# An expert's fourth block of outputs issued at the beginning of the next attention step, with the third norm's transposes ordered behind it

## The chip, the cores and the metric

The kernel runs on one core of a Trainium2 chip. Its time is the device time of one execution in microseconds (us). Five engines work side by side, each through its own instructions in their order: TensorE (PE, with its weight loads shown apart as PEld), VectorE (DVE), ScalarE (ACT), GpSimd (POOL) and SyncE (SP, which here only issues DMAs). They wait for each other by semaphores.

## What is computed

Two layers over 128 graphs of 64 nodes, 8192 nodes of 256 features in all, in float32. Each layer is a graph block and a feed-forward block, both with a residual:

```python
x = x + _L0_gnn_ref(_layernorm(x), adj, ...)     # graph convolution, softplus
x = x + _L0_ffn_ref(_layernorm(x), ...)          # 8 experts, the best one per node
x = x + _L1_gnn_ref(_layernorm(x), adj, ...)     # graph attention
x = x + _L1_ffn_ref(_layernorm(x), ...)          # 4 experts, the best two per node
...
def _L1_gnn_ref(h, adj, W, a, gamma, beta):
    Wh = jnp.matmul(h, W)
    e = s1[:, :, None] + s2[:, None, :]          # s1, s2 = Wh @ a1, Wh @ a2
    e = jnp.where(e > 0, e, ALPHA * e)
    e = jnp.where(adj > 0, e, NEG)
    attention = jax.nn.softmax(e, axis=2)
    h_prime = jnp.matmul(attention, Wh)
    return gelu(layernorm(h_prime) * gamma + beta)
...
    for ei in range(NUM_EXPERTS):                # in _L1_ffn_ref
        hh = jax.nn.gelu(x @ W1[ei] + b1[ei], approximate=False)
        out = out + g[..., None] * (hh @ W2[ei] + b2[ei])
```

The gate `g` of the last block comes from an attention over a list of 1,048,576 edges, whose sums need every node's row; so it is known late.

## The kernel before

The 8192 nodes are 64 tiles of 128, and four tiles are a group (16 groups). x stays on the chip throughout. The stages follow each other: layer 0's graph block and routing, layer 0's experts, then **attention's steps** (the stage of this change), then the edge list, and last the routed and remaining experts.

**The steps.** Attention runs in 26 steps (line 1322). In step s up to five generators, called streams, work each on its own group, so that a group passes through them in order: `back` (group s: fetches layer 0's expert rows by an indirect DMA on POOL, adds them to x on DVE, line 1168), `first` (group s-4: first norm, transposes, the products with W, the scores `ee`), `second` (group s-5: exponential `pb` on ACT line 1232, transposes of it on PE line 1236, copied to `pT` by ACT line 1238, the attention product on PE line 1243, copied into `ring` by ACT line 1244, then its statistics and `eps` on DVE lines 1145 and 1248), `combine` (group s-7: second norm on DVE lines 1260 and 1261, gelu, added to x), and `tables` (group s-10: third norm `z` on DVE line 1044, transposes on PE line 1184, copied to `zT` by ACT line 1185, stored, and eight small products for the edge list, line 1281). The streams take turns, one piece each per round r. At the end of every second step `make_factors` works out the norms' factors for two steps (the `mf` operations on DVE, lines 162 to 166, 1302, 1307 and 153 to 158).

**The units.** Beside the streams the last block's experts are already at work, on groups whose third norm is done: they fill TensorE's idle time, and what they make is stored in `ystore` until the gates are known. The generator `experts` hands out units of work. A hidden block is two products of 128x512 (line 1074) and a gelu on ACT (line 1078). An output block is four products of 128x256 into one `py` (line 1084, into the PSUM tile `pw`, of which there are two, shared with `first`), an addition of the bias on DVE (line 1088, into `yin`, of which there are six, shared with the rows that `back` fetches) and a store issued on SP (line 1111). An expert of a group is four hidden blocks and then four output blocks. In the profile each product of float32 shows as two matmul records, so an output block is eight records.

**The quota.** A line in the step loop says how many units are issued after each round of the streams. With at = s - 12, a step with an even `at` issues four units after the third round (the four hidden blocks of an expert), one with an odd `at` two after the first round and two after the second (its four output blocks). From step 21 on it is one after each of the first three rounds:

```python
                if s >= NG + SECOND:
                    quota = int(r < 3)
                elif at >= 0:
                    quota = (2 * (at % 2), 2 * (at % 2), 4 - 4 * (at % 2), 0, 0, 0, 0, 0)[r]
```

**The order.** The program is written as a stream of operations; a scheduler, at build time, decides each engine's order of instructions by priority (earlier written goes first) and by its own idea of what is ready, and sets the semaphores. `tc.issue_after(ins)` adds an edge for the scheduler alone: the instructions of its block come behind `ins` on the same engine.

Of the kernel before, what the change touches and what calls it, by code (L numbers as in the profile page):

```python
# [20 lines left out]
P = 128  # L21
# [3 lines left out]
GR = 4  # L25
# [3 lines left out]
FIRST, SECOND, COMBINE, TABLES = 2 * PART, 2 * PART + 1, 3 * PART + 1, 4 * PART + 2  # L29
RING = COMBINE - SECOND + 1  # L30
NG = NT // GR
# [49 lines left out]
def kernel(  # L81
# [31 lines left out]
    nc = tc.nc  # L113
# [30 lines left out]
    ident = const.tile([P, P], F32, name="ident")  # L144
# [273 lines left out]
    with tc.tile_pool(name="w0", bufs=1, reuse_waits="tile") as w0, tc.tile_pool(name="kp", bufs=1, reuse_waits="tile") as kp:  # L418
# [29 lines left out]
        with tc.tile_pool(name="b2", bufs=2, reuse_waits="tile") as b2, tc.tile_pool(name="bh", bufs=NH + 2, reuse_waits="tile") as bh, tc.tile_pool(  # L448
# [4 lines left out]
            def transposed(zT, z, k):  # L453
                tz = psb.tile([P, GR * P], F32, name="tz")[:, 0:D].rearrange("p (c n) -> p c n", c=2)
                for c in range(2):
                    nc.tensor.transpose(tz[:, c, :], z[:, c * P : c * P + P], ident)
                S.copy(zT[:, :, k * P : k * P + P], tz)
# [408 lines left out]
            with tc.tile_pool(name="bs", bufs=3, reuse_waits="tile") as bs, tc.tile_pool(  # L866
# [11 lines left out]
                steps, counts = keys.finish(bm), keys.count()  # L878
                zt_rows = zrows.rearrange("(s p) f -> s p f", p=P)
                why = "there are E0 experts, and no tile of theirs is past the last"  # L880

                def load(g):
# [23 lines left out]
                def turned(zs):  # L906
                    zT = b2.tile([P, 2, GR * P], F32, name="zT")
                    for k, z in enumerate(zs):
                        transposed(zT, z, k)
                    return zT  # L910
# [99 lines left out]
    def load_weights():  # L1010
        for e in range(NEXP):
            nc.sync.dma_start(w1[:, e], f1_w1[e].rearrange("(c p) f -> p c f", p=P))
            nc.sync.dma_start(w2[:, e], f1_w2[e].rearrange("(q p) f -> p q f", p=P))
        nc.sync.dma_start(b1, f1_b1.rearrange("e (q p) -> p e q", p=P))
        for t, of in ((b2, f1_b2.rearrange("e f -> (e f)")), (bgat, f1_bgat), (lng, f1_lng), (lnb, f1_lnb)):
            nc.sync.dma_start(t, row(of).to_broadcast(t.shape))
# [22 lines left out]
    def scaled(dst, src, g, norm, k):  # L1039
        scale, shift, mean = factors(g, norm, k)  # L1040
        if norm == 0:
            S.activation(dst, src, AF.Identity, bias=shift, scale=scale)
        else:
            V.tensor_scalar(dst, src, mean, scale, ALU.subtract, ALU.mult)
# [15 lines left out]
    adds = []  # L1060
    n_kept = [0] * DENSE
    pace = []
    sums = []
    behind = []

    def experts(g, take):

        zT = zTs.pop(g)
        for e in range(NEXP):
            hTs = []  # L1070
            for q in range(NH1):
                ph = to["ph"]()
                for c in range(2):
                    nc.tensor.matmul(  # L1074
                        ph, w1[:, e, c, q * P : q * P + P], zT[:, c, :], start=(c == 0), stop=(c == 1)
                    )
                hT = to["hT"]()
                pace[:] = [S, S.activation(hT, ph, AF.Gelu, bias=b1[:, e, q : q + 1]).ins]  # L1078
                hTs.append(hT)
                yield "h"  # L1080
            for k in range(GR):
                py = to["py"]()
                for q in range(NH1):
                    nc.tensor.matmul(  # L1084
                        py, hTs[q][:, k * P : k * P + P], w2[:, e, q, :], start=(q == 0), stop=(q == NH1 - 1)
                    )
                y = to["y"]()
                pace[:] = [V, V.tensor_tensor(y, py, b2[:, e * D : e * D + D], ALU.add).ins]  # L1088
                sums[:] = pace[1:]
                take(e, k, y)  # L1090
                yield "y"
# [10 lines left out]
    def dense():  # L1102

        for g in range(DENSE):

            def take(e, k, y):
                if adds:
                    adds[0](GR * g + k, e, y)
                else:
                    n_kept[g] = e + 1  # L1110
                    behind[:] = [nc.sync.dma_start(ystore[g, k, :, e * D : e * D + D], y).ins]

            if g == 0:
                prepare(0, to)
            for n, _ in enumerate(experts(g, take)):

                if n == (0 if to["two"] else NEXP * (NH1 + GR) - GR - 1) and g + 1 < DENSE and g + 1 not in zTs:
                    prepare(g + 1, to)
                yield (g, n)

    units = dense()

    with ExitStack() as of_c:
# [48 lines left out]
        def transposed(g, norm):  # L1172

            z = cz.tile([P, GR, D], F32, name="z")
            for k in range(GR):
                scaled(z[:, k, :], x[:, GR * g + k, :], g, norm, k)
            if norm == 2 and g >= DENSE:
                nc.sync.dma_start(zns[g - DENSE], z.rearrange("p k f -> p (k f)"))
            yield
            zT = c2.tile([P, 2, GR * P], F32, name="zT")  # L1180
            for c in range(2):
                tz = psc.tile([P, GR * P], F32, name="tz")
                for k in range(GR):
                    nc.tensor.transpose(tz[:, k * P : k * P + P], z[:, k, c * P : c * P + P], ident)
                S.copy(zT[:, c, :], tz)
            return zT

        def first(g):
            zT = yield from transposed(g, 0)
            yield  # L1190
            wh = whs[g % 2]
# [104 lines left out]
        def make_factors(i):  # L1296

            shape = [P, 3, PART * GR]
            raw = made["raw"]
            sm, df, ve, y, w = (c2.tile(shape, F32, name=f"mf{j}") for j in range(5))  # L1300
            moments(raw, sm, df, ve)
            V.tensor_tensor(ve, ve, made["eps"], ALU.add)
            fac = facs[i] = cf.tile([P, 3, 3, PART * GR], F32, name="fac")
            scale = fac[:, 0]
            root_of_bits(scale, ve, y, w)
            last = V.scalar_tensor_tensor(fac[:, 1], sm, -0.5, scale, ALU.mult, ALU.mult)
            V.tensor_scalar(fac[:, 2], sm, 0.5, None, ALU.mult)
            made["factors"] = last.ins
# [10 lines left out]
            }  # L1319
        )  # L1320
        g, n = 0, -1
        for s in range(n_steps):
            if s % PART == 0:
                made["raw"] = c2.tile([P, 3, PART * GR, 6], F32, name="raw")
                made["eps"] = c2.tile([P, 3, PART * GR], F32, name="eps")
                V.memset(made["raw"], 0.0)
                V.memset(made["eps"], EPS)
            streams = []
            for of, by_steps in ((back, 0), (combine, COMBINE), (tables, TABLES), (second, SECOND), (first, FIRST)):
                if 0 <= s - by_steps < NG:  # L1330
                    streams.append((of(s - by_steps), 2 if of == second and s % 2 else 0))
            if s == TABLES + 1:
                with tc.issue_after(made["sent"]):
                    load_weights()

            r = 0
            while streams:
                streams = [(st, at) for st, at in streams if at > r or next(st, s) is None]

                at = s - TABLES - 2  # L1340
                if s >= NG + SECOND:
                    quota = int(r < 3)
                elif at >= 0:
                    quota = (2 * (at % 2), 2 * (at % 2), 4 - 4 * (at % 2), 0, 0, 0, 0, 0)[r]
                else:
                    quota = 0
                for _ in range(quota):
                    g, n = next(units)
                r += 1
            if s % PART == PART - 1:  # L1350
                make_factors(s // PART)
        while (n + 1) % (NH1 + GR):
            g, n = next(units)
# [612 lines left out]
    with tc.tile_pool(name="gd", bufs=1, reuse_waits="tile") as gd:  # L1966
        steps = gates(gd, 0, T0, {})
        for _ in sending:
            next(steps, None)
            next(steps, None)  # L1970
            g, n = next(units)
        for _ in steps:
            pass
        while (n + 1) % (NH1 + GR):
            g, n = next(units)
# [179 lines left out]
```

## Time and profile before

| | us |
|---|---|
| median of 3 runs | 2231.14 (2227.64 to 2238.38) |
| the profiled execution | 2232.5 |
| its span, first to last instruction | 2230.4 |
| PE busy | 2067.0 (93%) |
| DVE busy | 1526.1 (68%) |
| ACT busy | 922.5 (41%) |
| POOL busy | 441.3 (20%) |

By stage, busy time of the engines, and the clock granted to TensorE:

| stretch of the span, us | what runs | PE busy | DVE busy | ACT busy | clock |
|---|---|---|---|---|---|
| 560 to 1100 | layer 0's experts | 537.5 of 540 | 441.4 | 111.1 | 1.00 |
| 1100 to 1269 | steps 0 to 12, no output blocks yet | 117.3 of 169 | 130.1 | 89.9 | 0.82 |
| 1269 to 1422 | steps 13 to 20, where the change is | 138.8 of 153 | 91.7 | 91.4 | 0.92 |
| 1422 to 1482 | the last steps | 59.9 of 60 | 45.8 | 20.4 | 1.00 |
| 1560 to 2230 | edge list and experts | 653.8 of 670 | 344.7 | 227.7 | 0.99 |

Busy shares are of the whole span or of the stretch; a busy PE is not PE at its peak. The granted clock is the share of full speed that TensorE was given. A line of the timeline is: start in us, how long it lasted, engine, source line, operation, tiles, shapes, number of records, and in brackets the idle time of the engine before it and what ended that.

### The profile page before, as it was taken

How to read it: one execution, taken by the hardware profiler on the slowest of the kernel's cores; microseconds unless marked ns; L12 is line 12 of the kernel's file. 1: busy time of each engine (PE TensorE's matmuls, PEld its weight loads, DVE VectorE, ACT ScalarE, POOL GpSimd, SP SyncE). 2: the span in 40 equal slices, each digit the busy share in tenths (PEclk: the TensorE clock that was granted, in tenths of full speed). 3: DMA queues.
4: the chain of work that ended last, by engine and by line, in shares of the span. 5: the costliest groups of instructions: out<-in, count | busy, mean ns of one | idle time of the engine just before them, and what ended most of it. 6: DMA issues, size and time to landing. Idle time of an engine off the chain costs nothing. (4 is left out here: it accounts for less than half of the span.)

```text
span 2230.4 us, 31413 instructions
## 1 busy us (share of the span) xinstructions
PE 2067.0 (93%) x10046; PEld 1387.5 (62%) x10046; DVE 1526.1 (68%) x4539; ACT 922.5 (41%) x1663; POOL 441.3 (20%) x464
## 2 busy tenths in 40 slices
PE   7899999897999999999867889998999999999999
PEld 5444444443667667666545666665667766888886
DVE  6998888924899999994178766665788742333435
ACT  4866767663221221222146655531333332333422
POOL 2011111112000000000052100003656653312214
PEclk9999999998999999999978998999999999999999
DMA  8121122222112111112122411172222236888943
GB/s 227 31 69 59 41 65 70 84 95 79 38 53 58 44 47 58 38 49 72 44 76 76 130 40 41 62 237 84 58 59 47 58 98 198 290 267 262 298 136 106
DMA packets 209212, 219.82 MB, mean 99 GB/s; under 512 B 55697, under 2 KB 176913, under 8 KB 209041
## 3 DMA queue, kind: packets, MB, share of 16 engines
q1 hardware_dynamic: 181296, 182.37, 26.7%
q0 software_dynamic: 16896, 35.05, 5.7%
q10 hardware_dynamic: 10848, 0.30, 0.3%
q8 instruction: 85, 1.39, 0.3%
q14 instruction: 87, 0.70, 0.1%
HBM read 132.66 MB, written 84.91 MB: 98 GB/s over the span
## 5 line engine op out<-in xcount | busy, mean ns | idle before, releaser
L466 PE MATMUL ph<-zT,w 128*128 128x512 f32 x1056 | 503.5, 607 | 14.9 <-ACT zT L699 11.3
L469 ACT ACTIVATE hT<-ph,b 128x512 f32<-128x512 f32 x264 | 180.5, 686 | 491.3 <-PE ph L466 487.2
L466 PEld LDWEIGHTS ph<-zT,w 128*128 128x128 f32 x1056 | 189.3, 192 | 195.6 <-issue 163.8
L933 PE MATMUL py<-wd,hT 128*128 x1088 | 250.6, 382 | 0.0
L296 DVE TENSOR_TENSOR one<-iota_l,pb 128x1024 bf16<-128x1024 bf16 x192 | 234.2, 1220 | 1.4 <-PE cnt_ps L307 1.4
L933 PEld LDWEIGHTS py<-wd,hT 128*128 128x128 f32 x1088 | 201.0, 190 | 24.8 <-issue 0.5
L1557 POOL DMA_INDIRECT got<-tsrc,esrc x144 | 166.4, 1155 | 209.2 <-DVE esrc L1528 86.8
L1084 PE MATMUL py<-w,hT 128*128 128x256 f32 x800 | 191.5, 390 | 11.0 <-DVE kt L1490 5.0
L1153 POOL DMA_INDIRECT yin<-yrows,row_y x64 | 63.5, 992 | 675.1 <-issue 571.1
L1074 PE MATMUL ph<-zT,w 128*128 128x512 f32 x400 | 186.6, 608 | 0.0
L1084 PEld LDWEIGHTS py<-w,hT 128*128 128x128 f32 x800 | 150.5, 193 | 41.8 <-issue 15.2
L1078 ACT ACTIVATE hT<-ph,b 128x512 f32<-128x512 f32 x100 | 68.6, 687 | 215.6 <-PE ph L1074 195.5
L2034 ACT ACTIVATE hT<-ph,b1e 128x256 f32<-128x256 f32 x152 | 71.9, 473 | 177.3 <-PE ph L2030 101.1
L2030 PE MATMUL ph<-zTp,w1e 128*128 128x256 f32 x608 | 140.0, 384 | 3.9 <-DMA w1e<-in_L_ffn_W_dram 3.9
L2051 DVE TENSOR_TENSOR y<-py,b2e 128x256 f32<-128x256 f32 x76 | 32.2, 424 | 157.3 <-PE py L2043 139.5
L2043 PE MATMUL py<-w,hT 128*128 x608 | 137.5, 379 | 0.0
L296 DVE TENSOR_TENSOR one<-iota_h,pb 128x512 bf16<-128x512 bf16 x192 | 131.9, 689 | 0.0
L2030 PEld LDWEIGHTS ph<-zTp,w1e 128*128 128x128 f32 x608 | 117.2, 193 | 20.5 <-issue 4.1
L625 PE MATMUL pre<-wd 128*128 128x512 f32 x256 | 126.5, 610 | 1.8 <-ACT wd L611 1.3
L2043 PEld LDWEIGHTS py<-w,hT 128*128 128x128 f32 x608 | 112.6, 190 | 13.8
L1074 PEld LDWEIGHTS ph<-zT,w 128*128 128x128 f32 x400 | 74.2, 193 | 73.1 <-issue 72.0
L755 POOL DMA_INDIRECT zrows<-z,pos x64 | 63.6, 994 | 278.3 <-issue 119.5
(409 smaller groups left out, 3471.1 us busy)
## 6 DMA issues: line engine op xcount, KB each, us to landing
w1e<-in_L_ffn_W_dram SPq DMA_DIRECT2D x38, 512.0 KB
yin<-ystore SPq DMA_DIRECT2D x24, 512.0 KB
ystore<-y SPq DMA_DIRECT2D x80, 128.0 KB
zslots<-none SPq DMA_DIRECT2D x38, 256.0 KB
zin<-zslots SPq DMA_DIRECT2D x38, 256.0 KB
yslots<-y SPq DMA_DIRECT2D x76, 128.0 KB
zin<-zrows SPq DMA_DIRECT2D x68, 128.0 KB
bd<-in_L_ffn_bd_dram SPq DMA_DIRECT2D x68, 128.0 KB
```

Of the source, the lines that this page charges most:

```text
L296: V.tensor_tensor(o, wi.unsqueeze(1).to_broadcast([P, HK, n]), pb[:, g : g + HK].unsqueeze(2).to_broadcast([P, HK, n]), ALU.is_equal,)
L466: nc.tensor.matmul(ph, w1[:, c, q * P : q * P + P], zT[:, c, :], start=(c == 0), stop=(c == 1))
L469: gelus.append(S.activation(hT, ph, AF.Gelu, bias=b1[:, q : q + 1]).ins)
L625: nc.tensor.matmul(pre, xnT[:, c, n * P : n * P + P], wcat[:, c, :], start=(c == 0), stop=(c == 1),)
L933: nc.tensor.matmul(py, hTs[q][:, k * P : k * P + P], wd[:, bass.ds(ex[k], 1), q, :].rearrange("p e f -> p (e f)"), start=(q == 0), stop=(q ...
L1074: nc.tensor.matmul(ph, w1[:, e, c, q * P : q * P + P], zT[:, c, :], start=(c == 0), stop=(c == 1))
L1078: pace[:] = [S, S.activation(hT, ph, AF.Gelu, bias=b1[:, e, q : q + 1]).ins]
L1084: nc.tensor.matmul(py, hTs[q][:, k * P : k * P + P], w2[:, e, q, :], start=(q == 0), stop=(q == NH1 - 1))
L1557: nc.gpsimd.indirect_dma_start(got, None, tsrc, bass.IndirectOffsetOnAxis(ap=esrc[:, b, at : at + 1], axis=0))
L2030: nc.tensor.matmul(ph, w1e[:, c, q * P : q * P + P], zT[:, c, :], start=(c == 0), stop=(c == 1))
L2034: pace[:] = [S, S.activation(hT, ph, AF.Gelu, bias=b1e[:, q : q + 1]).ins]
L2043: nc.tensor.matmul(py, hTs[q][:, k * P : k * P + P], w2[:, e, q, :].rearrange("p e f -> p (e f)"), start=(q == 0), stop=(q == NH1 - 1),)
```

## The change

In the odd `at` steps below step 21 (steps 13, 15, 17 and 19) only three output blocks are issued, two after the first round and one after the second. The fourth is issued at the very beginning of the following step (steps 14, 16, 18 and 20), before any stream of that step. The last product of it is kept as `held`, and while `held` is set the transposes of the third norm (`transposed` with norm 2, in the stream `tables`) are ordered behind it on TensorE. The number of units, of operations and of bytes is the same.

```diff
+    last_mm = []
...
-                    nc.tensor.matmul(
+                    mm = nc.tensor.matmul(
                         py, hTs[q][:, k * P : k * P + P], w2[:, e, q, :], start=(q == 0), stop=(q == NH1 - 1)
                     )
+                last_mm[:] = [mm.ins]
...
-                for k in range(GR):
-                    nc.tensor.transpose(tz[:, k * P : k * P + P], z[:, k, c * P : c * P + P], ident)
+                with tc.issue_after(held) if held is not None and norm == 2 else ExitStack():
+                    for k in range(GR):
+                        nc.tensor.transpose(tz[:, k * P : k * P + P], z[:, k, c * P : c * P + P], ident)
...
+        held = None
         for s in range(n_steps):
...
             r = 0
+            at = s - TABLES - 2
+            held = None
+            if at >= 2 and at % 2 == 0 and s < NG + SECOND:
+                g, n = next(units)
+                held = last_mm[0]
             while streams:
                 streams = [(st, at) for st, at in streams if at > r or next(st, s) is None]
-                at = s - TABLES - 2
+
                 if s >= NG + SECOND:
                     quota = int(r < 3)
                 elif at >= 0:
-                    quota = (2 * (at % 2), 2 * (at % 2), 4 - 4 * (at % 2), 0, 0, 0, 0, 0)[r]
+                    quota = (2 * (at % 2), at % 2, 4 - 4 * (at % 2), 0, 0, 0, 0, 0)[r]
```

## The prediction

> **What bounds the kernel now.** I read the page's busy shares, the stage windows, then the timelines of PE, DVE and ACT in the attention steps, and the wait list of PE there. TensorE is busy for 93% of the span and 59.85 of 60 us from 1422 on, so time can only be won where it stands idle or slow. In steps 13 to 20 that is in the even steps:
>
> ```profile
> PE tz L1184 <- DVE z L1044: 6.7, 3, 2.4
> PE p L1236 <- ACT pb L1232: 2.7, 4, 1.3
> PE ph L1243 <- ACT pT L1238: 2.0, 3, 0.7
> PE tz L1184 <- ACT zT L1185: 1.6, 3, 0.6
> PE ph L1243 <- DVE raw L1145: 0.7, 1, 0.7
> ```
>
> These are PE's waits between 1269 and 1422 us (total, times, longest): about 13.7 us. Steps 15 and 16 show where they lie:
>
> ```profile
> 1320.71 3.62 PE L1084 MATMUL pw<-w,hT 128*128 128x256 f32 x16
> 1324.16 1.86 PE L1281 MATMUL ph<-wgat,zT 128*128 128x24 f32 x16
> 1325.87 3.72 PE L1195 MATMUL pw<-wx,zT 128*128 128x257 f32 x16
> 1329.52 1.09 PE L1202 MATMUL p<-zT,w2r 128*64 128x256 f32 x8
> 1330.54 0.66 PE L1236 MATMUL p<-ident,pb 128*128 128x128 f32 x4
> 1331.87 2.30 PE L1243 MATMUL ph<-wh,pT 128*128 128x257 f32 x8 [0.67 <-ACT pT L1238]
> 1334.63 0.66 PE L1236 MATMUL p<-ident,pb 128*128 128x128 f32 x4 [0.46 <-ACT pb L1232]
> 1337.71 1.94 PE L1184 MATMUL tz<-ident,z 128*128 128x128 f32 x8 [2.42 <-DVE z L1044]
> 1340.15 1.11 PE L1184 MATMUL tz<-ident,z 128*128 128x128 f32 x4 [0.51 <-ACT zT L1185]
> ```
>
> The last two output blocks run back to back, nothing stands still until 1331.20, and then come four gaps. The long one ends on DVE, whose own order is what is late:
>
> ```profile
> 1335.01 0.17 DVE L1248 SCALAR_TENSOR_TENSOR eps<-ring 128x4 f32<-128x4 f32 x1 [0.41 <-ACT ring L1244]
> 1335.09 0.42 DVE L1145 BATCH_NORM_STATS2 raw<-ring 128x6 f32<-128x256 f32 x1
> 1335.55 0.20 DVE L162 TENSOR_TENSOR mf<-raw 128x24 f32<-128x24 f32 x1
> ...
> 1337.24 0.41 DVE L1044 TENSOR_SCALAR z<-x,fac 128x256 f32<-128x256 f32 x1
> ```
>
> So the third norm's z is queued behind the statistics of `ring`, which wait for the last attention product's copy. After each such gap the clock falls:
>
> ```profile
> core 0: us, PE busy (x) PEld busy (x) DVE busy (x) ACT busy (x) POOL busy (x), PEclk, DMA share, GB/s
> 1294.10:1304.40 10.30, 9.92 (x36) 8.90 (x37) 5.34 (x21) 3.90 (x8) 0.00 (x0) 0.50 0.17 56
> 1338.40:1348.80 10.40, 9.89 (x39) 8.50 (x38) 5.85 (x24) 2.99 (x6) 0.00 (x0) 0.51 0.16 54
> 1382.80:1386.30 3.50, 2.99 (x14) 2.22 (x15) 3.50 (x16) 1.37 (x3) 0.00 (x0) 0.51 0.36 150
> ```
>
> The seventh number is the granted clock: half speed for about 10.2, 10.2 and 3.4 us. From the transposes that wait for zT to the line 1202 products, the same work took 11.88 us in step 14 (1294.48 to 1306.36), 11.24 in step 16 (1340.15 to 1351.39) and 7.57 in step 18 (1385.26 to 1392.83): the longer stretches cost 4.3 and 3.7 us more than the short one.
>
> **The change part by part.** *Removed from the odd steps*: sixteen records from 1320.71 to the next group at 1324.16 are 3.45 us, so one block is 1.73 us. Everything behind it in the odd step starts 1.73 earlier; what it needs is there (line 1281 would start at 1322.43, its zT copies end at 1321.71; in steps 13 and 17 they end within 0.1 us of the need). Four blocks: 6.9 us, which is the most that can be won by filling.
>
> *Added to the even steps*: in the built program's order two of the block's four products come behind the first line 1236 transposes, the third in the middle of the line 1243 products, the fourth behind them, ahead of the second line 1236. In step 16, all shifted by 1.73: the first transposes end at 1329.47; two products (0.86) to 1330.33, where pT allowed 1330.14: 0.19 late. The four line 1243 products need 1.73 of their 2.30; the 0.57 inside are waits for `ring` copies, and the other two products (0.86) go there and into the 0.46. The second transposes start at about 1332.9, which is 1334.63 less 1.73: the block is absorbed up to there.
>
> *Queued behind it on ACT and DVE*: ACT now makes both pb before the last two `ring` copies; by their spacing of 0.43 the last copy ends near 1333.5, against 1334.97 less 1.73 = 1333.24: 0.26 lost. On DVE the block's bias addition (0.42 alone, 0.33 in a row of such) stands ahead of the `mf` operations and so of z: 0.33 lost. So the line 1184 transposes start 1.73 - 0.59 = 1.14 us earlier; PE then idles some 2.9 us before them, not 2.42. Steps 16 and 18: 1.14 each.
>
> *Step 14* is reordered more: row additions (0.48) and statistics (0.42) of `back` now stand between the first and the fourth z, which delays the fourth by about 0.7, while one row addition (0.39 in a row) leaves the path ahead of the first: 0.8 us won. *Step 20* has no `first`; expert products follow the second line 1236, so all idle time there can go: 0.68 and 0.47 seen plus 0.57 inside line 1243 is 1.72, less what z holds up later, at the least 1.14: I take 1.4. Sum: 0.8 + 1.14 + 1.14 + 1.4 = 4.5 us. Bounds: 0, if DVE's queue gives it all back, and 6.9.
>
> *Queues moved past.* SP issues the block's store behind the odd step's `tsrc` and ahead of `zts`, for which SP waits anyway from 1280.96 to 1294.95: nothing. In step 14 POOL's second gather for the last group reuses the block's buffer: DVE writes it near 1288.7, a store took 2.4 us until POOL went on (1273.92 to 1276.38), and three gathers at 1.25 end near 1295; their rows were added at 1312 to 1313, so some 15 us of other DVE work hide this. Without that cover DVE, and z behind it, would stand still.
>
> *The clock.* The idle stretch before the transposes stays, and is rather longer, so I expect half speed again after steps 14, 16 and 18; the lengths were 10.2, 10.2 and 3.4 us with nearly the same work behind. Bounds of the difference: 8 us less, if all are like step 18, and 2.7 + 3 x 1.7 = 7.8 more (step 18 like step 16, and one more 3.4 us piece at half speed each). I take 0.
>
> The Trainium skill (TensorE: Matmul & The Clock Gate, "HAM oscillation") says that the clock halves when TensorE idles for more than about 3.4 us. The trace has it halved after a gap of 2.42 us with shorter ones around it, so the measurement decides. By the page no gap of mine, at 2.9 us, would slow anything; if it held after the change, the half-speed time would go too, and the time would be nearer to the second case below.
>
> The profiled execution took 2232.5 us, so the sum gives 2228.0. It was 1.4 above the median of the three runs; at the median that is 2226.6, and I say 2227.
>
> **The rivals.** *The clock recovers sooner too* (20%): for it, step 18 shows that one piece of 3.4 us can be enough with the same work; against it, the long gap stays. 4.5 + 8 = 12.5: 2218.6 at the median.
>
> *The block only changes what PE waits behind* (13%): the additions of its bias and copies on DVE and ACT delay z by a whole block, and PE idles longer before line 1184. For it: z is what ends 6.7 of the 13.7 us. Against it: the 0.57, 0.67 and 0.46 before do not depend on z. It gives 0 to 1 us: 2230.6. That the change does nothing at all is excluded by the built order.
>
> *The half-speed stretches grow* (12%): gathering TensorE's idle time into one gap of 2.9 us starts the slow clock surely, and the sparse 24-column products behind it (line 1281: 3.02 us at half speed) keep it down. Price 7.8, less 4.5: 2234.4. It decides from the point where step 18's stretch is also 10 us long and one of the others more than 12. Against it: the work behind the gap is the same.
>
> **How the numbers follow.** The forecast, a gain of 2 to 7 us with the clock about as before, has 55%, and by itself 2223 to 2230. The runs before spread over 10.7 us. 0.5% is 11.2 us, about what a measurement of this kernel can tell from no change, so faster means under 2220.0 and slower over 2242.3. Faster: most of the clock's case and a few per cent of the forecast with a lucky spread, 0.24. Slower: only the last case with more than I can price, 0.08. Same: 0.68. The range takes in 2218.6 and 2234.4 with some spread: 2216 to 2236.
>
> **What would show it right or wrong.** Right: line 1281 follows the third output block 1.73 us earlier; no idle time ahead of line 1243 in steps 16 and 18; line 1088 directly ahead of the `mf` operations; an idle gap of 2.5 to 3 us before line 1184; PE idle between step 13 and 1422 down by about 4 us. Wrong: a gap over 3.5 us before line 1184, waits of DVE for gathers in step 14 or 15, or half-speed stretches that differ by over 5 us in sum from before. The stages behind 1482 should be as long as they were.

## The result, and the profile after

The changed kernel took 2232.83 us in the median of 14 runs (2225.24 to 2234.26). The kernel before, in as many runs beside it, took 2231.34 us (2223.50 to 2238.38). The ratio is 1.0000 with a 95% interval of 0.9987 to 1.0014: no difference, and a gain of 4.5 us (0.9980) lies outside the interval. The profiled execution took 2226.77 us, its span 2225.1. The lines of the steps have moved by 1 to 3: 1084 is now 1085, 1184 is 1187, 1195 is 1198, 1202 is 1205, 1236 is 1239, 1243 is 1246 and 1281 is 1284.

First PE's waits between 1269 and 1422 us (total, times, longest), the whole list:

```profile
PE tz L1187 <- DVE z L1044: 8.7, 4, 2.8
PE tz L1187 <- ACT zT L1188: 1.5, 3, 0.5
PE pw L1085 <- DVE yin L1090: 0.3, 1, 0.3
```

The waits for pb (2.7), pT (2.0) and ring's statistics (0.7) are gone, 5.4 us. The wait for z has grown from 6.7 to 8.7. With the wait for yin (0.3, in both), the list falls from 14.0 to 10.5: 3.5 us of waiting are won in all. The timeline of PE in steps 17 and 18 shows how:

```profile
1367.46 1.46 PE L1085 MATMUL pw<-w,hT 128*128 128x256 f32 x6
1368.76 1.86 PE L1284 MATMUL ph<-wgat,zT 128*128 128x24 f32 x16
...
1375.14 0.65 PE L1239 MATMUL p<-ident,pb 128*128 128x128 f32 x4
1375.63 1.03 PE L1085 MATMUL pw<-w,hT 128*128 128x256 f32 x4
1376.50 1.11 PE L1246 MATMUL ph<-wh,pT 128*128 128x257 f32 x4
1377.44 0.59 PE L1085 MATMUL pw<-w,hT 128*128 128x256 f32 x2
1377.87 1.03 PE L1246 MATMUL ph<-wh,pT 128*128 128x257 f32 x4
1378.74 0.59 PE L1085 MATMUL pw<-w,hT 128*128 128x256 f32 x2
1379.17 0.60 PE L1239 MATMUL p<-ident,pb 128*128 128x128 f32 x4
1382.53 1.93 PE L1187 MATMUL tz<-ident,z 128*128 128x128 f32 x8 [2.75 <-DVE z L1044]
1384.96 1.11 PE L1187 MATMUL tz<-ident,z 128*128 128x128 f32 x4 [0.51 <-ACT zT L1188]
...
1387.04 3.02 PE L1284 MATMUL ph<-wgat,zT 128*128 128x24 f32 x14
...
1396.35 1.09 PE L1205 MATMUL p<-zT,w2r 128*64 128x256 f32 x8
```

The eight records of the moved block stand where the prediction put them (4, 2 and 2 around line 1246), and no bracket is left between 1368.76 and the second line 1239. Nearly all idle time is now in one gap of 2.75 us, with the 0.51 for zT behind it. What follows it is slow: 3.02 us for the 14 records of line 1284, and 11.39 us from the transposes that waited for zT (1384.96) to line 1205 (1396.35), where the same work took 7.57 us before.

What ends the gap is DVE, here in step 16:

```profile
1336.58 0.42 DVE L1147 BATCH_NORM_STATS2 raw<-ring 128x6 f32<-128x256 f32 x1
1336.91 0.41 DVE L1090 TENSOR_TENSOR yin<-pw,b 128x256 f32<-128x256 f32 x1
1337.24 0.20 DVE L162 TENSOR_TENSOR mf<-raw 128x24 f32<-128x24 f32 x1
...
1338.93 0.41 DVE L1044 TENSOR_SCALAR z<-x,fac 128x256 f32<-128x256 f32 x1
```

The moved block's bias addition (line 1090) stands between the last statistics and the first `mf` operation and takes 0.33 us of its row (1336.91 to 1337.24). From those statistics to the first `mf` operation it is now 0.66 us; before it was 0.46 (1335.09 to 1335.55).

The clock, as windows over the three stretches at half speed (the columns are named in the first line; PEclk is the granted clock):

```profile
core 0: us, PE busy (x) PEld busy (x) DVE busy (x) ACT busy (x) POOL busy (x), PEclk, DMA share, GB/s
1294.80:1305.10 10.30, 9.45 (x37) 7.97 (x38) 7.89 (x30) 2.62 (x5) 2.60 (x3) 0.50 0.31 95
1339.20:1349.50 10.30, 9.60 (x39) 8.34 (x40) 6.74 (x28) 2.76 (x6) 0.00 (x0) 0.50 0.16 55
1383.50:1393.90 10.40, 9.89 (x38) 8.47 (x38) 5.57 (x22) 3.20 (x7) 0.00 (x0) 0.51 0.16 57
```

They belong to steps 14, 16 and 18. Before, they were 10.2, 10.2 and 3.4 us. Step 18's has tripled.

Both effects together, in one window of each kernel: from step 12's first hidden block (line 1074, now 1075) to step 20's. First the kernel before:

```profile
1260.20:1421.70 161.50, 146.51 (x679) 106.63 (x678) 100.15 (x323) 97.14 (x176) 7.72 (x8) 0.93 0.15 48
```

and the changed kernel:

```profile
1263.90:1423.50 159.60, 147.91 (x679) 109.84 (x678) 99.29 (x322) 96.41 (x174) 7.60 (x8) 0.90 0.14 48
```

The same 679 records; TensorE stands idle for 11.7 us instead of 15.0 but is busy for 1.4 us more, at a clock of 0.90 instead of 0.93. So 3.3 us of idle time went, 1.4 came back as more busy time, and 1.9 us were won in the steps of this execution. The slower work is more than the 1.4: the waits of 0.57 us inside each group of line 1243, which the block fills too, count as busy (2.30 us are listed there for 1.73 of work). The two profiled spans differ by 5.3 us; the other 3.4 lie outside the steps, and the medians show none of it.

### The profile page after: what moved, and what is told of

The parts are those of the page before. It is cut to its first block, busy times and chain, and to the rows that moved or that the text cites. A ratio compares the mean times of both kernels' runs of the same rounds, so it can differ in the third digit from the quotient of the medians.

```text
span 2225.1 us, 31413 instructions
## 1 busy us (share of the span) xinstructions
PE 2072.0 (93%) x10046; PEld 1395.4 (63%) x10046; DVE 1526.2 (69%) x4539; ACT 922.2 (41%) x1663; POOL 444.9 (20%) x464
## 5 line engine op out<-in xcount | busy, mean ns | idle before, releaser
L1085 PEld LDWEIGHTS py<-w,hT 128*128 128x128 f32 x800 | 151.1, 194 | 40.9 <-issue 14.9
```

The source lines that it names most:

```text
L1085: mm = nc.tensor.matmul(py, hTs[q][:, k * P : k * P + P], w2[:, e, q, :], start=(q == 0), stop=(q == NH1 - 1))
```

## The experiments

The runs were made on three chips, where the kernel before took 2211.51, 2210.89 and 2210.54 us in the median, some 20 us less than in the comparison above. So ratios to the kernel before on the same chip are compared, each with its 95% interval. Profiles of different chips are set beside each other only for their parts, the idle and the busy time of the same steps. My theory was that the move wins what its sum says at equal clock, and that TensorE's clock takes it back. The rival was that the block only changes what TensorE waits behind.

**The kernel before once more** (`before_again`), no edit: how far do two samples of one kernel differ, and is its profile typical?

> The kernel before, run again as a kernel of its own, for the granted clock of each of its runs. Theory (clock): filling the even steps' idle time is worth about 4.5 us at equal clock, and half-speed stretches after steps 14, 16 and 18 that are longer than before take it back; then the runs of before have a mean clock above the 0.9645 of the changed kernel's runs, by 0.001 to 0.003 (each 3.4 us piece of half speed is 0.0008 of clock), and its profile has less than 30 us of half speed between 1269 and 1425. Rival (given back later): the clock is the same, 0.964 to 0.965, and the gain goes in a wait behind 1425 us. Time: ratio 1.000 to itself.

2209.22 us (12 runs), ratio 0.9994 (0.9984 to 1.0004). The clock of its runs was 0.967 to 0.970, above the 0.9655 to 0.9675 expected; but it was another chip than that of the changed kernel's runs. Its stretches in steps 16 and 18 were 10.2 and 3.4 us, as in the first profile, and in step 14 13.7: with the three together at 27.3 us the bound of 30 held.

**The changed kernel on a second chip** (`after_again`), no edit:

> The changed kernel unchanged, on the same chip as the three runs below. Theory (the move is worth about 4.5 us at equal clock, and the half-speed stretches of the attention's steps grow by as much): ratio 0.9985 to 1.0015, mean granted clock of its runs 0.003 to 0.005 below that of the kernel before on this chip. Rival (the block only changes what TensorE waits behind, and the clock does not matter): the same ratio, but the same clock within 0.001.

2211.01 us (11 runs), ratio 1.0003 (0.9994 to 1.0012). The mean clock of its runs was 0.9666 (0.966 to 0.968), of the 21 runs of the kernel before beside it 0.9683 (0.966 to 0.970): lower by 0.0017, in the direction expected, but little more than half of the least expected. That is some 7.5 us more at half speed in 2210 (0.0017 x 2210 / 0.5). The windows from step 12 to step 20, of before_again:

```profile
1253.90:1415.70 161.80, 146.90 (x679) 107.12 (x678) 100.10 (x323) 97.02 (x175) 7.70 (x8) 0.92 0.14 48
```

and of after_again:

```profile
1252.50:1414.80 162.30, 150.50 (x679) 111.37 (x678) 99.89 (x322) 96.72 (x175) 7.60 (x8) 0.89 0.14 47
```

Again less idle time, by 3.1 us (11.8, not 14.9), and here 3.6 us more busy with the same 679 records. Step by step, between the first hidden blocks of the steps named (start of line 1074 or 1075):

| stretch | before | after | before_again | after_again | won, both pairs | forecast |
|---|---|---|---|---|---|---|
| step 12 to 16 | 92.19 | 89.74 | 92.41 | 91.99 | 2.45, 0.42 | 0.8 + 1.14 |
| step 16 to 18 | 41.44 | 43.73 | 41.45 | 44.09 | -2.29, -2.64 | 1.14 |
| step 18 to 20 | 27.81 | 26.11 | 27.82 | 26.12 | 1.70, 1.70 | 1.4 |
| sum | 161.44 | 159.58 | 161.68 | 162.20 | 1.86, -0.52 | 4.5 |

The row of step 18 is the turn. Its half-speed stretch was 3.41 us in both profiles of the kernel before and 10.24 in both of the changed one. Without a stretch of its own, in step 20, the move won 1.70 us both times.

**Useless products in the long gap** (`spare_block`): the changed kernel, with four products, which nobody reads, behind the second line 1239 of steps 14, 16, 18 and 20 (`made["tp"]` is the last transpose of that line). More work, and no other wait removed.

```diff
+            made["tp"] = mm.ins
...
+                if r == 1 and held is not None:
+                    with tc.issue_after(made["tp"]):
+                        spare = to["py"]()
+                        for q in range(NH1):
+                            nc.tensor.matmul(spare, ident, w2[:, 0, q, :], start=(q == 0), stop=(q == NH1 - 1))
```

> The changed kernel with one more block of four products, of data that is there and into a PSUM tile that nobody reads, behind the second line 1236 transposes of steps 14, 16, 18 and 20: 1.73 us of TensorE work that computes nothing, in the 2.76 us gap. Theory (clock): the gap falls to about 1.0 us, no half-speed stretch follows steps 14, 16 and 18, and each saves about 4 us, so 8 to 12 us less than before (0.995 to 0.996) in spite of 6.9 us more products. Rival (the clock costs nothing, since DVE or ACT sets the pace there): no less than before, 1.000 to 1.001. Rival (the gap's length isn't what sets the clock): half-speed stretches stay, 1.000.

2201.04 us, ratio 0.9951 (0.9938 to 0.9965): 10.8 us less, with 32 more records on the engine that is the bound. The clock of its runs rose to 0.972 to 0.976. Its timeline in step 16, with the useless products at line 1363 and line 1284 moved to 1285:

```profile
1322.40 0.60 PE L1239 MATMUL p<-ident,pb 128*128 128x128 f32 x4
1322.84 1.89 PE L1363 MATMUL pw<-w,ident 128*128 128x256 f32 x8
1325.76 1.68 PE L1187 MATMUL tz<-ident,z 128*128 128x128 f32 x8 [1.04 <-DVE z L1044]
...
1329.16 1.64 PE L1285 MATMUL ph<-wgat,zT 128*128 128x24 f32 x14
```

The gap is 1.04 us instead of 2.76, and line 1285's products take 1.64 us, not 3.02. z came no earlier (3.36 us from the second line 1239 to line 1187, as in the changed kernel), so within these steps nothing but the clock can have paid for the added work. From step 12 to 20 the window is 157.4 us (shown below), 4.9 less than that of after_again, with as much busy time (150.3 and 150.5) for 32 more records; the rest of the 10.8 us lies outside these steps and isn't explained by the profiles. Against the theory, stretches of 6.8 us in step 14 and 10.2 us in step 18 stayed, behind gaps of 1.03 us.

**The same products in the kernel before** (`before_spare`): what is the move worth, with the long gap filled in both?

> The kernel before, its fourth block where it was, with the same four useless products behind the second L1236 of steps 14, 16, 18 and 20 as in spare_block. Set beside spare_block (ratio 0.9951) it prices the move with the long gap shortened in both. Theory: the clock rises as in spare_block, the waits ahead of L1243 stay empty, so 3 to 5 us slower than spare_block: ratio 0.9965 to 0.9975. Rival (the move is worth nothing whatever the clock): as fast as spare_block, 0.995.

2207.41 us (11 runs), ratio 0.9991 (0.9982 to 1.0001), clock 0.971 to 0.974. So the useless products gained 0.1% here, and none is not excluded; the window below is 3.3 us shorter than that of before_again. The move, then, is worth the distance from 0.9991 to 0.9951, 0.4% or 8.8 us, with some 3.6 us of uncertainty from the two intervals. That is against the rival, and more than my 3 to 5. The two profiled spans are only 2.0 us apart (2203.6 and 2201.6), the windows below 1.1, so the size stays open. Its windows from step 12 to 20, and below them those of spare_block, show the parts:

```profile
1250.90:1409.40 158.50, 148.47 (x711) 107.95 (x710) 101.46 (x333) 97.46 (x175) 8.33 (x11) 0.97 0.15 49
```

```profile
1250.70:1408.10 157.40, 150.31 (x711) 111.35 (x710) 101.15 (x333) 97.12 (x175) 8.22 (x11) 0.95 0.15 49
```

Idle 10.0 us without the move, 7.1 with it: 2.9 us less, much as in the first two pairs, and again partly paid for in clock (0.97 to 0.95).

**The moved block in the long gap instead** (`in_the_gap`): no block at the beginning of the step; the fourth is issued behind the second line 1239.

```diff
...
             if at >= 2 and at % 2 == 0 and s < NG + SECOND:
-                g, n = next(units)
                 held = last_mm[0]
...
+                if r == 1 and held is not None:
+                    with tc.issue_after(made["tp"]):
+                        g, n = next(units)
```

> The fourth block isn't issued at the beginning of the even step but behind its second line 1236 transposes, that is in the long gap before line 1184; the waits for pT and ring copies (1.7 us in each even step) stay. Theory (clock): the gap falls to about 0.7 us, half speed doesn't follow, so 5 to 6 us of filling and 8 to 9 us of clock: 13 us less than before, 0.994. Rival (clock costs nothing): 5 us less at the most, 0.998. Rival (given back later): 1.000.

2204.49 us, ratio 0.9964 (0.9950 to 0.9979): 8.0 us less, not 13. The waits for pT and pb came back (2.0 and 2.6 us in its list), and stretches of 10.2 us stayed in steps 16 and 18, though no idle piece there was longer than 0.7 us. Step 18, and the window of its stretch:

```profile
1366.33 1.68 PE L1187 MATMUL tz<-ident,z 128*128 128x128 f32 x8 [0.70 <-DVE z L1044]
1368.62 0.83 PE L1187 MATMUL tz<-ident,z 128*128 128x128 f32 x4 [0.61 <-ACT zT L1188]
```

```profile
1368.90:1379.30 10.40, 10.40 (x38) 9.18 (x37) 5.74 (x22) 4.28 (x8) 0.00 (x0) 0.51 0.15 48
```

So half speed doesn't need the long gap, and the theory that the gap alone sets the clock is refuted. The same block, moved to the other place of the same step, is worth 8 us rather than none.

**A block in both places** (`two_blocks`): the third at the beginning of the even step, the fourth in the gap.

```diff
...
-                    quota = (2 * (at % 2), at % 2, 4 - 4 * (at % 2), 0, 0, 0, 0, 0)[r]
+                    quota = (2 * (at % 2), 0, 4 - 4 * (at % 2), 0, 0, 0, 0, 0)[r]
...
+                if r == 1 and held is not None:
+                    with tc.issue_after(made["tp"]):
+                        g, n = next(units)
```

> The third block goes to the beginning of the even step, as the fourth did in the change, and the fourth into the long gap behind the second line 1236 transposes. Theory (clock): 4.5 us as forecast for the first, some 5 us more of the gap filled, and 8 to 9 us of half speed gone: 17 us less than before, 0.992. Rival (clock costs nothing): 9 us less, 0.996. Rival (given back later): 1.000.

2200.65 us, ratio 0.9961 (0.9946 to 0.9976): 8.6 us less by the ratio, half of what was expected. Steps 16 and 18 kept full speed, but the gap ahead of line 1187 was still 1.0 us, step 14 had its 10.2 us, and step 13 got a stretch of 3.4 us behind a wait of 1.1 us for zT. It cannot be told from in_the_gap by these intervals.

**z made a step earlier** (`z_before` and `z_after`): the third norm's z of an even step is made by DVE in the odd step before it, so that it no longer queues behind `ring`'s statistics. The edit is the same in both kernels.

```diff
+        early = []
...
-                    streams.append((of(s - by_steps), 2 if of == second and s % 2 else 0))
+                    if of == tables and early:
+                        streams.append((early.pop(), 1))
+                    else:
+                        streams.append((of(s - by_steps), 2 if of == second and s % 2 else 0))
...
+                if r == 2 and TABLES + 3 <= s < NG + SECOND - 1 and s % 2:
+                    early.append(tables(s + 1 - TABLES))
+                    next(early[0])
```

> The kernel before, but the third norm's z of an even step is made on VectorE in the odd step before it. Theory: in steps 14 to 20 no gap of over 1 us is left ahead of L1184, no half-speed stretch of 10 us is left between 1285 and 1425 us, and the time is 8 to 15 us less: ratio 0.993 to 0.9965. Rival (the half speed comes from the thin work itself, not from the gap): stretches stay, ratio 0.998 to 1.

> The changed kernel with the third norm's z of an even step made in the odd step before it. Theory: no gap is left for the moved block to leave behind, so its own gain shows: 1 to 4.5 us less than z_before; the lower end because in z_before the third norm's transposes now fill the waits ahead of L1243 as well. Rival (the move is worth nothing): as z_before within 1 us.

z_before took 2186.22 us, ratio 0.9890 (0.9875 to 0.9905), z_after 2184.42, ratio 0.9885 (0.9870 to 0.9900): 24 and 25 us less, well over the 8 to 15 expected. PE's waits from 1253 to 1400 us in z_after are, complete:

```profile
PE p L1075 <- ACT hT L1079: 1.6, 2, 0.8
PE pw L1085 <- DVE yin L1090: 0.3, 1, 0.3
```

and from step 12 to step 20 the windows of z_before and of z_after read:

```profile
1252.00:1393.50 141.50, 138.38 (x689) 101.54 (x688) 101.23 (x327) 96.81 (x177) 7.79 (x8) 0.99 0.18 59
```

```profile
1253.90:1391.90 138.00, 135.49 (x689) 100.10 (x687) 101.04 (x334) 97.07 (x177) 7.89 (x9) 1.00 0.18 59
```

Against before_again (161.8 us, 14.9 idle, 146.9 busy) z_before has 3.1 us idle and 138.4 busy: 11.8 us less idle, since the third norm's transposes, ready early, also fill the waits for pT, and 8.5 less busy, with ten more records in the window. So making z earlier was worth 20 us in these steps, where the list of waits showed 6.7 for it. Of the 23.1 us between the two profiled spans (2207.3 and 2184.2) these are 20.3; what made the rest was not traced. One stretch of 3.4 us is left, in step 18: it begins at 1357.86, and in the 20 us before it no idle piece of TensorE was longer than 0.23 us.

**The pair once more** (`z_after_2`, `z_before_2`), for the small difference between them:

> z_after once more, for the difference of the pair. Theory (with the long gap gone the moved block still saves the wait for the third norm's z no longer, but the waits of its own): 1 to 4.5 us less than z_before_2, ratio to the kernel before 0.9885. Rival (nothing is left to gain): within 0.5 us of z_before_2.

> z_before once more: ratio 0.989 by both theories; the difference from z_after_2 tells them apart.

2183.53 and 2186.22 us, ratios 0.9877 (0.9858 to 0.9895) and 0.9887 (0.9870 to 0.9905). Over both pairs, eight runs of each, z_after is 2.1 us faster in the mean, with a standard error of 1.0. So the lower half of 1 to 4.5 is likely; no difference at all is not quite excluded. The windows above say where it is: 0.6 us less idle, and 2.9 less busy. The one stretch of 3.4 us that z_before has at 1358 is not in z_after, which is worth at most 1.7 of the 2.9; the other 1.2 is not explained. z_after is the fastest kernel of the study, 1.2% under the kernel before.

The second part of the change, the ordering of the transposes behind the moved block, was not run by itself. The traces show only that it was not what the transposes waited for: they came 2.75 us behind the block's and line 1239's products, and z released them (1382.53 in step 18).

## Why the prediction was right, and where it was not

- **The time** (2227 us, forecast of a gain too small to measure): 2232.83 lies within 2216 to 2236, and the verdict is no difference. But the 4.5 us that the sum promised did not arrive in the time, and the case that had 55%, a gain of 2 to 7 us with the clock about as before, did not come. The time lies in the range because the range took in the rivals too; so it is right with one step wrong.
- **"Everything behind it in the odd step starts 1.73 earlier"; "the block is absorbed up to there"**: right. Line 1284 follows the third block at once, and no bracket is left until the second line 1239. TensorE's idle time fell by 3.1 to 3.3 us, against about 4 named as a sign.
- **"Steps 16 and 18: 1.14 each"**: undersized. Line 1284 to line 1187 took 13.77 us in each (1325.62 to 1339.39; 1368.76 to 1382.53). In the kernel before, line 1281 less one block (1322.43) to line 1184 (1337.71) is 15.28: 1.51 won each. After_again gives the same. So z came only 0.22 later than the block's 1.73 would have it, not 0.59: the addition on DVE takes 0.33 but moves the `mf` operations by 0.20, and the copies of `ring` cost nothing that shows. The gap grew from 2.42 to 2.76, not to 2.9.
- **Step 20, "I take 1.4"**: 1.70 in both pairs, of the 1.72 seen.
- **Step 14, 0.8**: 0.70. From line 1284 to the transposes that waited for zT took 17.13 us (1280.33 to 1297.46); before, from line 1281 less one block (1276.65) to 1294.48, 17.83. What followed cannot be separated, since the order behind these transposes changed too; with step 16 the row gave 2.45 and 0.42 against the 1.94 of the forecast. The sum itself was thus a little small: 0.70 + 1.51 + 1.51 + 1.70 is 5.4 in the first pair, where the rows gave 1.86.
- **"The clock ... I take 0"**: this is the step that failed. The signs I gave for it said so: the stretches of steps 14 to 18 differ by 6.8 us in sum (23.9 to 30.7), over the 5 that I had named as wrong. Step 18, with 1.51 us won ahead of its transposes, lost 2.29 and 2.64 in total: the clock took 3.8 and 4.15 us there. My price for that step alone was 2.7; the lines behind it were in the prediction already, 7.57 us for the short stretch and 11.24 for a long one, which is 3.7. In the second pair the row of steps 14 and 16 has 0.42, where 0.89 and 1.51 were won up to their transposes; so some 2 us more went there, at stretches as long as in before_again, and what took them was not found.
- **The rivals**: that the stretches grow (12%) was the mechanism, halfway: step 18's became 10 us, and none of the others grew from before to after in either pair (step 14's 13.65 us in after_again, over the 12 that I had named, was in before_again too). So it paid back the gain and little more; its 2234.4 is no further from 2232.83 than the measurement can tell. That the clock recovers sooner (20%) is refuted by both profiles. That the block only changes what TensorE waits behind (13%) forecast the time better than mine did (2230.6), and falls by the waits: 2.9 to 3.3 us less idle in three pairs.
- **"The stages behind 1482 should be as long as they were"**: not quite. The stretch near 1520 to 1530 is 6.8 us in both profiles of before and 10.2 in both of after, worth at most 1.7 us; one at 1486 grew from 3.4 to 6.8 in the first pair alone.

I weighed the clock by what the gap would do if it stayed, and gave the change of its length the middle of two bounds. What was not seen is that the clock can take as much as the filling wins. Why step 18's stretch tripled stays open: the gap ahead of it grew by only 0.33 us, and half speed also came where no idle piece was over 0.7 us (in_the_gap).

## What to carry to other kernels

On an engine that is the bound, idle time has two prices: its own length, and what the clock does to the work behind it. Here the wait for z was 6.7 us long, and making z earlier won about 20: 11.8 of idle time, since other waits were filled with it, and 8.5 of busy time. Before filling the small gaps ahead of a long one, look at what ends the long one: making its operand earlier on an engine with time to spare was worth 24 us, a block moved in front of it nothing. And compare windows over the same records, with the granted clock beside them: here busy time rose by 1.4 and 3.6 us for the same 679 records while the clock fell by 0.03.

## What was unexpected of the hardware

Useless products made the changed kernel 0.5% faster (ratio 0.9951, where the changed kernel itself has 1.0003). In the kernel before, they gained 0.1% (0.9991), and none is not excluded.

The half speed comes in pieces of 3.41 us: stretches of 3.41, 6.83, 10.24 and 13.65 us occur in steps 13 to 20 of these runs and no others. Their beginnings lie whole pieces apart (in the first profile of the kernel before 44.37 us, 13 pieces, from step 14 to 16 and from 16 to 18), while the steps do not, so the pieces fall differently on the same work. Between one piece and three the following reading fits what was seen, but was not tested. In step 18 of both profiles of the kernel before, the stretch begins 0.05 us after the transposes that waited for z, so that its first piece holds nearly nothing but transposes, and the clock is back behind it. Where it began 0.17 us ahead of them, or 0.78 to 1.95 us behind (steps 16 and 18 otherwise), the thin products of line 1281 or 1284 fall into the first and second piece, and three pieces followed. If it is so, then the change moved step 18 off a lucky place, and another small shift could do the same with no change of work.

The Trainium skill (TensorE: Matmul & The Clock Gate, "HAM oscillation") lets the clock halve once TensorE idles for more than about 3.4 us. No gap of these steps was longer than 2.76 us in any run here; half speed followed every one of 2.4 to 2.8 us, and two of the three of about 1.03 us in spare_block, with shorter ones beside them. It also came with none over 0.7 us, in steps 16 and 18 of in_the_gap and step 16 of before_spare. The same page ("A second HAM failure mode") tells of a kernel in which frequent short idle pieces between groups of products do it too; the traces here agree with that, but no run shows what decides between half and full speed: z_before's stretch came with no piece over 0.23 us.
